# Two biases of a deformable-convolution block: three-row products on TensorE, or an add on VectorE as the products are copied to SBUF

## The chip, the cores and the metric

The kernel runs on one core of one Trainium2 chip. The metric is the time of one execution on the device in microseconds. Before the change it was 2654.45 us, the median of three runs (2650.62 to 2654.76).

## The reference

One layer with a deformable convolution, an attention layer and an expert layer, over x of 8 x 56 x 56 x 128 in fp32. The change touches the end of the first:

```python
y = dcn_core(xp, offset, mask) @ w_out + b_out
x = x + gamma1 * layer_norm(y, ln1_g, ln1_b)
m = gelu(x @ w_fc1 + b_fc1) @ w_fc2 + b_fc2
x = x + gamma2 * layer_norm(m, ln2_g, ln2_b)
```

Then causal self-attention over the 3136 tokens of an image (128 wide) is added to x, and then a layer of 64 experts, each of which takes the 8 tokens of an image with the largest gate values.

## The kernel before

**Work and order.** Each image's tokens are cut into four groups of 896 or 448 tokens, 7 or 4 tiles of 128 (the last of a 448 group half full); there are 32 groups. A group passes through some twenty *lines* of steps, written as generators: `prepare` (transposes, the input product), `conv` (depthwise taps on VectorE, L576), `plan` and `weigh` (tap weights; their product with the sampled rows on VectorE, L715), `sums` (folds of these products on GpSimd, L732), `project`, `norm`, `scores`, `maxes` (score evictions on VectorE, L1092), `exps`, `turn`, `pour`, `attend`, `mix` and `after`. All lines of all groups are interleaved by one long string, `ORDER`: each letter advances one line by one step, and the steps' instructions are put on the engines' queues in that order. Each engine works its queue in order. The string came out of a search by a planner, which works with the costs in `need(engine, us, ...)`; `lock=True` marks VectorE steps that it takes to exclude GpSimd. On the chip these costs do nothing. After the last `project` the experts' tiles take the place of the first stage's; the experts' products and the scatters to the output close the program.

**`project`.** A group's tiles are taken in banks of three or four (one PSUM bank of 512 columns). For each bank:

1. `py` = bias + yT x `w_out`, in the PSUM tile `held` (L841: the bias; L843: one product for each tile, which runs as two instructions).
2. `add_normed`, through `deviations`: ScalarE squares each tile of `py` with a sum over the columns (L784), GpSimd makes of the sums the reciprocal standard deviations (L786 and `power`, L775), ScalarE scales the tiles into `u` (L796), TensorE transposes them (L801), VectorE scales and adds them to `xT` (L803).
3. The two layers of 512: products with `fc1` (L856) and GELU (L863); then `pm` = bias + products with `fc2`, again in `held` (L875: the bias; L877).
4. `deviations` of `pm`; for each tile VectorE multiplies it with its deviation and with `grow`, the row of gains, into `u` (L897); VectorE adds `u` to the transposed `xT` and stores it in `t` (L907).

The means need no step: `settle` takes the mean over the columns off `w_out`, `fc2` and both biases beforehand (`centered`). It also splits each bias into three bf16 rows whose sum is the fp32 value (L442, L443, L446); the bias comes into PSUM as a product of these three rows with three rows of ones:

```python
nc.tensor.matmul(py[:, : m * C], three, b_out[:, : m * C], start=True, stop=False)
```

There are 7 banks to an image, 56 in all, of which 24 hold three tiles and 32 four; and 200 tiles. Other lines that will be named: L543, where VectorE adds the bias of the input product as it copies that product from PSUM to SBUF; L1240, which adds the attention's result to `t`; L1387 and L1477, which add gathered rows up in SBUF, weighted; L1406, L1378, L621, L645 and L648, small VectorE steps on tiles in SBUF; L1140, the exponential of the scores in SBUF; L1998, the load of a bias row to many partitions near the end.

## Time and profile before

| | |
|---|---|
| runs | 2654.76, 2654.45, 2650.62 us |
| profiled execution | 2649.75 us, span 2647.7 us |
| mean granted TensorE clock | 0.979 |
| DMA | 442.63 MB, mean 167 GB/s |
| tap products (L715) | 200 x 3.48 us on VectorE |
| folds (L732) | 1075 on GpSimd, 1419.7 us |
| products of the attention (L1203) | 5200 instructions, 681.4 us on TensorE |

The profile shows one execution of the program. The span runs from its first instruction to its last; the execution's time is 2.05 us longer. Busy times are of the engine's own instructions; a wait for a semaphore ahead of an instruction is not part of them, but what an instruction waits for after it has begun is. In a line of a group stand: line, engine, operation, out<-in by the program's names, out<-in sizes, how many; then busy us, mean ns of one; then how long the engine stood idle just before them, and what ended most of that. In a line of the waits stand: who waited, for whom, us in total, times, longest us. A line of the program in order of time begins with its start and its length in us.

### The profile page before, as it was taken

How to read it: one execution, taken by the hardware profiler on the slowest of the kernel's cores; microseconds unless marked ns; L12 is line 12 of the kernel's file. 1: busy time of each engine (PE TensorE's matmuls, PEld its weight loads, DVE VectorE, ACT ScalarE, POOL GpSimd, SP SyncE). 2: the span in 40 equal slices, each digit the busy share in tenths (PEclk: the TensorE clock that was granted, in tenths of full speed). 3: DMA queues.
4: the chain of work that ended last, by engine and by line, in shares of the span. 5: the costliest groups of instructions: out<-in, count | busy, mean ns of one | idle time of the engine just before them, and what ended most of it. 6: DMA issues, size and time to landing. Idle time of an engine off the chain costs nothing. (4 is left out here: it accounts for less than half of the span.)

```text
span 2647.7 us, 47634 instructions
## 1 busy us (share of the span) xinstructions
PE 2467.3 (93%) x16297; PEld 1883.2 (71%) x16297; DVE 2166.3 (82%) x4661; ACT 1943.2 (73%) x4524; POOL 2179.0 (82%) x2315
## 2 busy tenths in 40 slices
PE   4789999999999999999999899999999999999975
PEld 3677777777776778777776667766777777777744
DVE  6988877899898987888889897888889988765553
ACT  2356787888787887888778577977888887876630
POOL 3686889889998899989899899987998899882245
PEclk9799999999999999999999999999999999999987
DMA  5665544544553454444454354544465445335083
GB/s 163 204 226 203 203 169 159 193 129 164 188 187 124 161 193 176 173 150 167 169 182 153 123 199 170 181 149 151 160 202 172 146 167 191 132 94 197 23 280 117
DMA packets 274296, 442.63 MB, mean 167 GB/s; under 512 B 14332, under 2 KB 127356, under 8 KB 274044
## 3 DMA queue, kind: packets, MB, share of 16 engines
q1 hardware_dynamic: 184220, 382.09, 41.2%
q10 hardware_dynamic: 86464, 50.94, 6.3%
q0 software_dynamic: 3360, 6.45, 0.8%
q8 instruction: 132, 2.16, 0.3%
q14 instruction: 120, 0.98, 0.1%
HBM read 386.04 MB, written 53.48 MB: 166 GB/s over the span
## 5 line engine op out<-in xcount | busy, mean ns | idle before, releaser
L732 POOL TENSOR_TENSOR g<-g 128x128 f32<-128x128 f32 (+6 forms) x1075 | 1419.7, 1329 | 104.0 <-DVE g L715 25.4
L715 DVE TENSOR_TENSOR g<-g,tp 128x3200 f32<-128x3200 f32 (+1 forms) x200 | 695.2, 3478 | 17.7 <-ACT tp L706 10.8
L1203 PEld LDWEIGHTS av<-v,pe 128*128 128x128 f32 (+2 forms) x5200 | 626.4, 188 | 97.3 <-issue 60.1
L1203 PE MATMUL av<-v,pe 128*128 128x129 f32 (+2 forms) x5200 | 681.4, 277 | 2.8 <-ACT pe L1173 1.5
L1066 PE MATMUL sc<-zT,qT 128*128 128x384 f32 (+8 forms) x1622 | 657.7, 516 | 16.9 <-DVE S L1092 8.2
L1092 DVE TENSOR_SCALAR_CACHE_REDUCE S<-sc 128x512 f32<-128x512 f32 (+5 forms) x783 | 443.4, 576 | 209.5 <-PE sc L1066 121.8
L1140 ACT ACTIVATE S<-S,low 128x512 f32<-128x512 f32 (+5 forms) x783 | 478.7, 638 | 42.9 <-DVE low L1108 31.1
L1173 ACT COPY pe<-tr 128x512 f32<-128x512 f32 (+3 forms) x775 | 379.8, 500 | 143.9 <-PE tr L1158 111.1
L1158 PE MATMUL tr<-ident,S 128*128 128x128 f32 x2516 | 392.5, 276 | 12.6 <-DVE S L1092 9.5
L1158 PEld LDWEIGHTS tr<-ident,S 128*128 128x128 f32 x2516 | 297.4, 142 | 130.3 <-issue 68.5
L1066 PEld LDWEIGHTS sc<-zT,qT 128*128 128x128 f32 (+1 forms) x1622 | 247.0, 187 | 113.2 <-issue 43.4
L576 DVE SCALAR_TENSOR_TENSOR pv<-xg,dw,pv 128x448 f32<-128x448 f32 x448 | 305.8, 683 | 14.0 <-ACT pv L573 8.3
L877 PEld LDWEIGHTS pm<-fc,hid 128*128 128x128 f32 x1600 | 200.3, 193 | 37.7 <-issue 22.6
L877 PE MATMUL pm<-fc,hid 128*128 128x128 f32 x1600 | 222.4, 282 | 1.5 <-POOL hid L862 1.0
L856 PE MATMUL ph<-xT,fc 128*128 128x512 f32 (+2 forms) x448 | 207.4, 551 | 6.0 <-DVE xT L803 4.0
L863 ACT ACTIVATE hid<-ph,b_fc 128x512 f32<-128x512 f32 (+2 forms) x224 | 140.7, 633 | 97.0 <-PE ph L856 93.9
L667 POOL TENSOR_TENSOR taps<-taps,a 128x252 f32<-128x252 f32 (+1 forms) x288 | 191.3, 664 | 8.8
L657 POOL TENSOR_TENSOR a<-w 128x756 f32<-128x756 f32 (+1 forms) x96 | 136.4, 1420 | 20.9 <-DVE w L648 18.4
L1140 ACT ACT_TABLE_LOAD x87 | 111.6, 1283 | 6.0 <-DVE pv L576 3.7
L760 ACT COPY ys<-ptg 128x128 f32<-128x128 f32 (+1 forms) x200 | 52.4, 262 | 84.9 <-PE ptg L749 43.0
L749 PE MATMUL ptg<-ident,g 128*128 128x128 f32 (+1 forms) x650 | 85.0, 292 | 25.1 <-POOL g L732 25.0
L749 PEld LDWEIGHTS ptg<-ident,g 128*128 128x128 f32 (+1 forms) x650 | 81.8, 207 | 29.2 <-POOL g L732 27.6
(328 smaller groups left out, 3716.0 us busy)
## 6 DMA issues: line engine op xcount, KB each, us to landing
g<-img SPq DMA_DIRECT2D x192, 1600.0 KB
w1t<-in_L_ffn_weight_dram SPq DMA_DIRECT2D x32, 512.0 KB
w2t<-in_L_ffn_weight_dram SPq DMA_DIRECT2D x32, 512.0 KB
xin<-in_x_dram SPq DMA_DIRECT2D x56, 224.0 KB
xTd<-xc ACTq DMA_DIRECT2D x56, 224.0 KB
img<-st ACTq DMA_DIRECT2D x112, 112.0 KB
out_dram<-t ACTq DMA_DIRECT2D x24, 448.0 KB
g<-img SPq DMA_DIRECT2D x8, 800.0 KB
```

Source lines behind the costliest of these rows:

```text
L576: nc.vector.scalar_tensor_tensor(p3, src, dw[:, k : k + 1], p3, op0=ALU.mult, op1=ALU.add)
L667: nc.gpsimd.tensor_add(dst, dst, a5[:, :nt, kx])
L715: nc.vector.tensor_mul(g3, g3, tp[:n, lt % 4].unsqueeze(2).to_broadcast([n, NTAP * NG, 32]))
L732: nc.gpsimd.tensor_add(g[:n, o * C : (o + w) * C], g[:n, o * C : (o + w) * C], g[:n, i * C : (i + w) * C])
L856: nc.tensor.matmul(ph[:, :n], fc1[:, f * P : (f + 1) * P], xT[:, :n], start=True, stop=True)
L877: nc.tensor.matmul(four(pm, m)[:, i, :], h[:, i * P : (i + 1) * P], fc2[:, f, :], start=False, stop=i == m - 1 and f == 3,)
L1066: nc.tensor.matmul(pp[h * HALF : h * HALF + qw, c0 : c0 + m], qT[:, q0 : q0 + qw], zTs[b, g][:, k0 : k0 + m], start=True, stop=not seg.las ...
L1092: nc.vector.tensor_scalar(S[p0:p1, c0:c1], pp[p0:p1, c0:c1], -SCALE, None, ALU.mult, ALU.min, accum_out=(mn[p0:p1, i, j + k : j + k + 1] i ...
L1140: nc.scalar.activation(S[p0:p1, c0:c1], S[p0:p1, c0:c1], AF.Exp, bias=low[p0:p1, i : i + 1], scale=-1.0)
L1158: nc.tensor.transpose(pt[:m, k + p0 : k + w], S[p0:w, k : k + m], ident[p0:w, p0:w])
L1173: nc.scalar.copy(pe[:, : full * P], pt[:, : full * P])
L1203: nc.tensor.matmul(p3[h * HALF : h * HALF + qw, i % 3, :], pe[:kw, k + h * HALF : k + h * HALF + qw], vs[b, g][:kw, (k0 + k - c0) // P, :] ...
```

## The change

`raw_b` holds both biases in fp32 on all 128 partitions. The three-row products, and what prepares them, are gone. After `py` is done, and again after `pm`, a new step `biased` adds the bias on VectorE and writes `y` in SBUF; Square and the scaling on ScalarE, and the multiply by `grow` on VectorE, read `y` where they read PSUM. `u` is now `y` itself, in place; the squares go to a tile of their own. `ORDER` is another string throughout.

```diff
 ORDER = (
-    "ppppbpppppppwbpwwpppwvvfvvvvvvvvbppwcpccccckpwcccpccpccpbpppwfccwvccvccvccvvvccvwwcccvfvcgvg"
...
+    "ppppbppppppwpwpppwpvvvvvvbvvbvvpwcppwcbcccccfppcwwcccpppcpcpvwcvvwcccvvwvcccwvcvcvfvvcvwfvvb"
...
-    raw_b = wk.tile([3, 2, C], F32, tag="oT", name="raw_b")
+    raw_b = sp.tile([P, 2, C], F32, tag="b3", name="raw_b")
     for k, n in enumerate(("L0_conv_b_out", "L0_conv_b_fc2")):
-        nc.sync.dma_start(raw_b[:, k], a[n].partition_broadcast(3))
+        nc.sync.dma_start(raw_b[:, k], a[n].partition_broadcast(P))
...
-    three = cst.tile([3, P], BF16, tag="three", name="three")
-    nc.gpsimd.memset(three, 1.0)
-    less = cst.tile([3, 2], F32, tag="less", name="less")
-    nc.gpsimd.memset(less, -1.0)
-    nc.gpsimd.memset(less[:1, 0:1], 0.0)
-    nc.gpsimd.memset(less[:2, 1:2], 0.0)
-    b3 = sp.tile([3, 2, 4 * C], BF16, tag="b3", name="b3")
-    b_out, b_fc2 = b3[:, 0], b3[:, 1]
...
         for k in range(2):
             yield need(DVE, 1.4)
-            v = raw_b[:, k]
-            centered(v, 3, 5 + k)
...
+            centered(raw_b[:, k], P, 5 + k)
...
     def deviations(pb, name):
...
-        u = sp.tile([P, 4, C], F32, tag="u", name="u" + name)
         for i in range(m):
-            nc.scalar.activation(u[:, i], pb[:, i, :], AF.Square, accum_out=ss[:, i : i + 1])
+            square = sp.tile([P, C], F32, tag="square", name=f"square{name}_{i}")
+            nc.scalar.activation(square, pb[:, i, :], AF.Square, accum_out=ss[:, i : i + 1])
...
-        return ss, u
+        return ss
...
     def add_normed(xT, pb, name):
...
-        ss, u = yield from deviations(pb, name)
+        ss, u = (yield from deviations(pb, name)), pb
...
+    def biased(pb, k, m, name):
+
+        yield need(DVE, 0.15 + 0.135 * m)
+        y = sp.tile([P, 4, C], F32, tag="y", name="y" + name)
+        nc.vector.tensor_add(y[:, :m], four(pb, m), raw_b[:, k].unsqueeze(1).to_broadcast([P, m, C]))
+        return y[:, :m]
...
-            yield need(PE, 0.22 + 0.224 * m, since=[there, None])
+            yield need(PE, 0.115 * m, since=[there, None])
             py = ps.tile([P, 512], F32, tag="held", name=f"py{nm}_{i0}")
-            nc.tensor.matmul(py[:, : m * C], three, b_out[:, : m * C], start=True, stop=False)
             for i in range(m):
                 nc.tensor.matmul(
                     four(py, m)[:, i, :],
                     yT[:, (i0 + i) * P : (i0 + i + 1) * P],
                     w_out,
-                    start=False,
-                    stop=i == m - 1,
-                )
-            yield from add_normed(xT[:, :n], four(py, m), f"a{nm}_{i0}")
+                    start=True,
+                    stop=True,
+                )
+            y = yield from biased(py, 0, m, f"a{nm}_{i0}")
+            yield from add_normed(xT[:, :n], y, f"a{nm}_{i0}")
...
-                turned[f] = yield need(PE, 0.224 * m + 0.22 * (f == 0), since=at)
+                turned[f] = yield need(PE, 0.224 * m, since=at)
...
-                    nc.tensor.matmul(pm[:, : m * C], three, b_fc2[:, : m * C], start=True, stop=False)
...
-                        start=False,
+                        start=f == 0 and i == 0,
...
-            ss, u = yield from deviations(four(pm, m), f"b{nm}_{i0}")
+            y = yield from biased(pm, 1, m, f"b{nm}_{i0}")
+            ss, u = (yield from deviations(y, f"b{nm}_{i0}")), y
             for i in range(m):
                 yield need(DVE, 0.345)
                 nc.vector.scalar_tensor_tensor(
                     u[:, i, :],
-                    four(pm, m)[:, i, :],
+                    y[:, i, :],
                     ss[:, i : i + 1],
                     grow,
```

## The prediction

> **What bounds the kernel now.** I read the busy shares first, then the table by stage, then the groups of the operations that the change touches, then single instructions in order of time. The shares over the whole span:

> ```profile
> PE 2467.3 (93%) x16297; PEld 1883.2 (71%) x16297; DVE 2166.3 (82%) x4661; ACT 1943.2 (73%) x4524; POOL 2179.0 (82%) x2315
> ```

> The first bias product starts at 97 us and the last at 2394 us, so the stretch that counts is 100 to 2400 us. The table by stage gives, after the stretch's limits and length, the busy time of TensorE, its weight loads, VectorE, ScalarE and GpSimd, then the granted clock. The second and third lines are the two 100 us stages in which VectorE was busiest.

> ```profile
> 100.00:2400.00 2300.00, 2224.00 (x14373) 1697.85 (x14373) 1963.57 (x4113) 1808.38 (x4240) 2038.26 (x2107) 0.99 0.49 168
> 100.00:200.00 100.00, 87.41 (x599) 72.93 (x598) 92.29 (x116) 49.82 (x136) 78.28 (x70) 0.94 0.63 224
> 2000.00:2100.00 100.00, 96.27 (x639) 72.43 (x638) 92.11 (x229) 80.58 (x197) 88.22 (x99) 1.00 0.42 138
> ```

> TensorE is busy for 2224/2300 = 96.7% of it: it is the bound, at a granted clock of 0.99. VectorE stands at 85.4% and GpSimd at 88.6%, not far behind, and no 100 us stage shows VectorE above 92.3%. The chain that ended last shows only the final scatters and says nothing of this stretch.

> **The change, part by part.** There are 7 banks to an image, 56 in all; 24 hold three tiles and 32 hold four, 200 tiles together. Each bank passes both layer norms.

> *Products taken off TensorE.* 112 three-row products go. Their groups (busy us, mean ns of one, idle before them):

> ```profile
> L875 PE MATMUL pm<-b,three 3*128 3x512 bf16 x32 | 12.5, 391 | 0.0
> L841 PE MATMUL py<-b,three 3*128 3x512 bf16 x32 | 12.5, 391 | 0.6 <-DVE ub L897 0.6
> ...
> L875 PE MATMUL pm<-b,three 3*128 3x384 bf16 x24 | 7.9, 331 | 0.0
> L841 PE MATMUL py<-b,three 3*128 3x384 bf16 x24 | 7.9, 331 | 0.7 <-DVE ub L897 0.7
> ```

> That is 2 x (12.5 + 7.9) = 40.8 us of TensorE, all on the bounding engine, so 41 us is the most that the change can win. The bank `held` comes free sooner; TensorE waited 0.6 + 0.7 us for that, which I cost at nothing.

> *Adds put on VectorE.* Each reads a product from PSUM and a bias row from SBUF and writes SBUF. That is the form of L543, and nearly that of L907, so the second and the fourth of these lines price it. The other two price a thing that the diff does in passing: the multiply by `grow` (L897) reads `y` in SBUF where it read `pm` in PSUM, so that both its tensors now lie in SBUF. L1387 is the same operation at the same size with both in SBUF.

> ```profile
> L897 DVE SCALAR_TENSOR_TENSOR ub<-pm,ssb,grow 128x128 f32<-128x128 f32 x200 | 59.4, 342 | 28.8 <-POOL ssb L775 28.8
> ...
> L543 DVE TENSOR_TENSOR st<-pq,b_in 114x512 f32<-114x512 f32 x56 | 38.3, 684 | 25.7 <-PE pq L538 25.5
> ...
> L1387 DVE SCALAR_TENSOR_TENSOR po<-gx,chances,po 128x128 f32<-128x128 f32 x21 | 21.0, 999 | 0.0
> ...
> L907 DVE TENSOR_TENSOR t<-ub,pt 128x384 f32<-128x384 f32 x32 | 17.6, 549 | 0.5
> ```

> The adds: 2 x (32 x 0.684 + 24 x 0.549) = 70.1 us.

> *The multiply.* L897 takes 342 ns and L1387 takes 999. In order of time the reason stands side by side (start us, us):

> ```profile
> 862.06 1.12 DVE L897 SCALAR_TENSOR_TENSOR ub<-pm,ssb,grow 128x128 f32<-128x128 f32 x4
> 863.09 2.84 DVE L1387 SCALAR_TENSOR_TENSOR po<-gx,chances,po 128x128 f32<-128x128 f32 x1
> ```

> ```profile
> 862.35 3.44 POOL L732 TENSOR_TENSOR g<-g 128x1536 f32<-128x1536 f32 x1
> ```

> Four multiplies with a PSUM operand run through a GpSimd fold undisturbed. The one with two SBUF operands ends at 865.93, with the fold (865.79). Its shortest is 337 ns, its median 529, its longest 3341: the work is no longer, it waits for GpSimd's instruction in flight. GpSimd is busy for 88.6% of the stretch, and right ahead of these multiplies, since they follow its `pow`. Price: 200 x (0.999 - 0.342) = 131.4 us of VectorE. Bounds: at the end, where GpSimd has little to do, the same form (L1477) takes 411 ns on average, which makes 200 x 0.069 = 14 us; if each waits for a mean GpSimd instruction (2179.0/2315 = 0.94 us), 188 us. I take 131, the row with the same form, engine and stage. GpSimd in turn: a 128x128 fold right behind such a multiply (855.42 us) took 507 ns against a mean of 460, so 200 x 0.05 = 10 us; if each multiply held it for its whole length, 68 us.

> [...]

> *ScalarE.* Square and the scaling read SBUF, not PSUM. A 512-wide activation takes 725 ns from SBUF (L1140) and 686 from PSUM (L863): 600 x 39 ns = 23 us, on an engine with 78.6% of the stretch. I cost it at nothing; uncovered it is 23 us.

> [...]

> *The wait that is added.* Square waited for TensorE and now waits for the add, which stands in VectorE's queue among score evictions (L1092), convolution taps (L576) and tap products (L715); behind Square wait the two small GpSimd steps. GpSimd already stands idle for it:

> ```profile
> POOL ssb L786 <- ACT ub L784: 61.3, 29, 9.8
> ```

> The other lines' work hides one more step of 0.6 us in each of 112 norms as long as VectorE is on time. I cost it at nothing; without cover it is 112 x 0.63 = 70 us.

> *The start.* `raw_b` comes in over 128 partitions instead of 3, on SP's queue in its old place; a like broadcast load near the end took SP 1.9 to 3.2 us to issue (L1998), so at most 5 us later for what stands behind it. Five GpSimd memsets and 4.8 us of VectorE's splitting (1.4 + 2.3 + 1.1) go. TensorE is busy for 45 of the first 100 us and waits for other things: nothing either way.

> *The order.* All engines' queues get another order. Nothing in the trace prices that. It can win at most TensorE's idle time of the stretch, 76 us, and I bound a loss by the same; I take zero and keep some 40 us on each side for the range. What speaks for the losing side: the planned costs of the new code give the multiply 0.345 us with no lock, and the `py` product 0.115 us a tile where L843 was busy for 60.5 us over 200 tiles, 0.30 each.

> **The sum.** VectorE in the stretch: 1963.6 + 70.1 + 131.4 = 2165 us, 94.1% of 2300. Two ways on from there.

> By capacity: the busiest stages show 92%. At 92% throughout, 2165 us need 2353 us, +53; at 90%, 2406, +106.

> By what reaches TensorE: 1460 to 1490 us is a place with many such waits.

> ```profile
> 1460.00:1490.00 30.00, 23.08 (x131) 15.80 (x129) 27.52 (x48) 18.37 (x46) 28.39 (x29) 1.00 0.43 136
> ```

> ```profile
> L1406 DVE TENSOR_SCALAR slot_f<-at_f 32x8 f32<-32x8 f32 x4 | 4.1, 1021 | 0.1
> ...
> L645 DVE TENSOR_TENSOR om<-om,red 128x252 f32<-128x252 f32 x1 | 3.5, 3458 | 0.0
> ```

> Besides these five, L621 took 2.55 us and L1378 2.28. Undisturbed they take 0.16 us (the shortest L1406, taken for L1378 too) and 0.42 (the median L645, taken for L621 too), so the seven lost 3.4 + 3.0 + 2.1 + 2.1 = 10.6 us. TensorE was busy for 23.1 us where its mean share gives 29.0: 5.9 lost, 0.56 of the wait. So 0.56 x 131.4 = +74. The adds are no waits and alone would bring VectorE to 88.4%: nothing. Of the 41 us saved I count half, because TensorE now waits for VectorE more often: -20. Sum +54.

> The two ways give +53 to +106. I take +60: the profiled execution (2649.75 us, span 2647.7) becomes 2709.8, and as it lies 4.7 us below the median of the runs, the median becomes 2714.

> **The rivals.**
> *VectorE becomes the bound outright* (10%): each multiply waits for a whole GpSimd instruction (+188) and the queue reaches only 90%: (1963.6 + 70 + 188)/0.9 = 2469, +169, some 2820. For it: four multiplies run in a row, and the next fold can get in between them. Against: L1387 runs between other work too and shows a median of 529.

> *Faster* (16%): the multiplies meet GpSimd in its pauses, or between short steps, as L1477 does with 411 ns. VectorE then carries 70 + 14 us more, 88.9%, TensorE stays the bound and gives back 40.8 x 0.967 = 39 us: 2615. It decides for this side where the mean of the 200 multiplies stays below about 0.45 us. Against it: GpSimd has 11% of the stretch free, and the multiply follows GpSimd's own step.

> *Gain and loss cancel* (4%): about half the price of the waits, within 0.2% of before, which is about what a measurement of this kernel can tell from no change. That the products stay is excluded: the diff deletes them.

> **How the numbers follow.** Slower as forecast 70%, VectorE as the bound 10%: slower 0.80; same 0.04; faster 0.16. The main case by itself reaches from 2660 (a good order) to 2775 (+106 and some of the order). From 2625 to 2810 the range leaves out most of the fastest rival and the upper half of the slowest, under 2 in 10.

> **What would show it.** The multiply's group: about 1.0 us on average with a shortest of 0.34, many ending with a GpSimd fold; the adds at 0.68 and 0.55 without spread; VectorE near 2365 us in all and above 92% in many stages; TensorE 41 us less busy, but more of its idle time ended by VectorE. Wrong if the multiply's mean is below 0.45 us, or if VectorE holds 94% and TensorE does not slow.

## The result, and the profile after

The changed kernel takes 2785.4 us (median of four runs, 2784.15 to 2786.36) against 2652.8 us before: 132.6 us more, a ratio of 1.0509 with an interval of 1.0496 to 1.0521. The forecast was +60. The direction and the mechanism that it named are there; the size is more than twice what it gave. The profiled execution took 2785.58 us (span 2783.7), at a mean granted clock of 0.962 where it was 0.979.

The busy shares of the changed kernel:

```profile
PE 2479.5 (89%) x16185; PEld 1904.4 (68%) x16185; DVE 2363.3 (85%) x4763; ACT 1993.8 (72%) x4524; POOL 2190.0 (79%) x2311
```

VectorE did 197 us more, within 2 us of the 2365 us that the prediction worked out. TensorE has the 112 products fewer (x16185 for x16297), but instead of 41 us less it was busy for 12 us *more*. That is the line to be puzzled by: fewer instructions, more time. Its idle time grew from 180.4 us (2647.7 - 2467.3) to 304.2.

The table by stage of the changed kernel, same columns as before; the second and third line are the two 100 us stages with the busiest VectorE:

```profile
100.00:2550.00 2450.00, 2249.46 (x14318) 1727.20 (x14319) 2168.82 (x4247) 1869.13 (x4263) 2050.88 (x2110) 0.97 0.46 158
200.00:300.00 100.00, 91.23 (x620) 75.12 (x619) 92.79 (x137) 58.40 (x142) 65.44 (x52) 0.97 0.53 189
700.00:800.00 100.00, 94.08 (x615) 73.40 (x615) 93.22 (x172) 78.75 (x180) 91.73 (x89) 1.00 0.50 175
```

VectorE carries 2168.82 us of its stretch, but the stretch has grown with it: 88.5% of 2450, not the 94.1% of the old length. Four of the 24 stages from 100 to 2500 us lie above 92% (before: two), where the prediction looked for many. No engine is full; the kernel is slower although every engine but VectorE has more room than before.

The groups of the multiply and of the four-tile adds after the first product (busy us, mean ns of one, idle before them):

```profile
L886 DVE SCALAR_TENSOR_TENSOR yb<-yb,ssb,grow 128x128 f32<-128x128 f32 x200 | 222.9, 1157 | 18.7 <-POOL ssb L757 17.5 <-ACT pe L1162 1.2
...
L801 DVE TENSOR_TENSOR ya<-py,raw_b 128x512 f32<-128x512 f32 x32 | 21.9, 686 | 17.2 <-PE py L831 17.0
```

The adds are as priced: 0.69 us here and 0.55 for three tiles, all between 0.54 and 0.70. With the pair after `pm` they take 70.3 us. The multiply is not: 1157 ns on average where 342 stood, with a shortest of 311, a median of 754 and a longest of 3593. Of the 200, 150 took over 450 ns, and each of those ended within 0.16 us behind the end of a GpSimd instruction (median 0.15).

The longest waits show who is late now:

```profile
POOL ssa L768 <- ACT squarea L766: 117.3, 40, 8.6
...
POOL ssb L768 <- ACT squareb L766: 65.0, 38, 7.3
```

Before, the second stood at 61.3 us and the first here:

```profile
POOL ssa L786 <- ACT ua L784: 41.3, 23, 7.3
```

TensorE's own waits rose from 152.7 to 275.2 us; those ended by VectorE from 54 to 127.5.

**One such wait from start to end.** VectorE, the changed kernel, in order of time (start us, us):

```profile
905.84 1.37 DVE L886 SCALAR_TENSOR_TENSOR yb<-yb,ssb,grow 128x128 f32<-128x128 f32 x1
...
907.20 6.42 DVE L886 SCALAR_TENSOR_TENSOR yb<-yb,ssb,grow 128x128 f32<-128x128 f32 x3
913.54 0.68 DVE L1081 TENSOR_SCALAR_CACHE_REDUCE S<-sc 128x512 f32<-128x512 f32 x1
```

GpSimd in the same microseconds:

```profile
905.51 1.55 POOL L639 TENSOR_TENSOR a<-w 128x756 f32<-128x756 f32 x1
907.03 7.39 POOL L714 TENSOR_TENSOR g<-g 128x1536 f32<-128x1536 f32 x5
```

TensorE behind them:

```profile
908.61 0.81 PE L1055 MATMUL sc<-zT,qT 128*128 128x384 f32 x2
...
909.92 0.49 PE L1147 MATMUL tr<-ident,S 128*128 128x128 f32 x3
914.28 1.65 PE L1055 MATMUL sc<-zT,qT 128*128 128x384 f32 x2 [3.87 <-DVE S L1081]
```

The first multiply ends just behind GpSimd's `a` product, and the next three wait among its five folds: 7.8 us for what takes 1.4 undisturbed. The score eviction (L1081) queued behind them comes late, and TensorE, which waits for it, stands for 3.87 us. Then comes the part that the prediction did not see: the same two score products that took 0.81 us take 1.65. The table by stage of the same place says why (the granted clock is the sixth figure behind the stage's length, those in brackets not counted):

```profile
910.00:914.20 4.20, 0.41 (x4) 0.17 (x2) 4.20 (x6) 1.02 (x2) 3.96 (x5) 0.86 0.41 159
914.20:921.00 6.80, 6.72 (x22) 4.04 (x23) 6.12 (x22) 4.13 (x14) 3.15 (x7) 0.59 0.00 0
921.00:926.00 5.00, 5.00 (x28) 3.27 (x28) 3.78 (x12) 2.77 (x5) 4.92 (x3) 1.00 0.61 225
```

Behind the pause TensorE is "busy" for 6.72 of 6.80 us at a clock of 0.59, with 22 instructions where the 5 us after it hold 28. The pause is paid twice: once as idle time, and once as a stretch at half speed (a granted clock of 0.50 until 919.83 us) that counts as busy.

### The profile page after: what moved, and what is told of

It is laid out like the page before. It is cut to its first block, busy times and chain, and to the rows that moved or that the text cites. A ratio compares the mean times of both kernels' runs of the same rounds, so it can differ in the third digit from the quotient of the medians.

```text
span 2783.7 us, 47363 instructions
## 1 busy us (share of the span) xinstructions
PE 2479.5 (89%) x16185; PEld 1904.4 (68%) x16185; DVE 2363.3 (85%) x4763; ACT 1993.8 (72%) x4524; POOL 2190.0 (79%) x2311
## 5 line engine op out<-in xcount | busy, mean ns | idle before, releaser
L1055 PE MATMUL sc<-zT,qT 128*128 128x384 f32 (+8 forms) x1622 | 675.3, 526 | 64.2 <-DVE S L1081 32.4
L1192 PEld LDWEIGHTS av<-v,pe 128*128 128x128 f32 (+2 forms) x5200 | 637.9, 191 | 109.3 <-issue 57.7
L1192 PE MATMUL av<-v,pe 128*128 128x129 f32 (+2 forms) x5200 | 694.2, 280 | 8.7 <-ACT pe L1162 7.8
L1081 DVE TENSOR_SCALAR_CACHE_REDUCE S<-sc 128x512 f32<-128x512 f32 (+5 forms) x783 | 442.7, 576 | 146.8 <-PE sc L1055 97.6
L1147 PE MATMUL tr<-ident,S 128*128 128x128 f32 x2516 | 402.2, 279 | 45.3 <-DVE S L1081 13.1
L886 DVE SCALAR_TENSOR_TENSOR yb<-yb,ssb,grow 128x128 f32<-128x128 f32 x200 | 222.9, 1157 | 18.7 <-POOL ssb L757 17.5
L865 PE MATMUL pm<-fc,hid 128*128 128x128 f32 x1600 | 215.5, 278 | 3.2 <-ACT hid L852 2.8
L852 ACT ACTIVATE hid<-ph,b_fc 128x512 f32<-128x512 f32 (+2 forms) x224 | 141.2, 634 | 67.9 <-PE ph L845 64.5
L731 PE MATMUL ptg<-ident,g 128*128 128x128 f32 (+1 forms) x650 | 91.3, 306 | 27.2 <-POOL g L714 26.0
```

What stands on the lines that cost most here:

```text
L865: nc.tensor.matmul(four(pm, m)[:, i, :], h[:, i * P : (i + 1) * P], fc2[:, f, :], start=f == 0 and i == 0, stop=i == m - 1 and f == 3,)
L886: nc.vector.scalar_tensor_tensor(u[:, i, :], y[:, i, :], ss[:, i : i + 1], grow, op0=ALU.mult, op1=ALU.mult,)
L1055: nc.tensor.matmul(pp[h * HALF : h * HALF + qw, c0 : c0 + m], qT[:, q0 : q0 + qw], zTs[b, g][:, k0 : k0 + m], start=True, stop=not seg.las ...
L1081: nc.vector.tensor_scalar(S[p0:p1, c0:c1], pp[p0:p1, c0:c1], -SCALE, None, ALU.mult, ALU.min, accum_out=(mn[p0:p1, i, j + k : j + k + 1] i ...
L1147: nc.tensor.transpose(pt[:m, k + p0 : k + w], S[p0:w, k : k + m], ident[p0:w, p0:w])
L1192: nc.tensor.matmul(p3[h * HALF : h * HALF + qw, i % 3, :], pe[:kw, k + h * HALF : k + h * HALF + qw], vs[b, g][:kw, (k0 + k - c0) // P, :] ...
```

## The experiments

The theory: the multiply's second SBUF operand makes it wait for GpSimd, and that alone costs most of the time. The rivals: the new order is worse whatever it orders (prediction: zero, within 40 us); the adds load VectorE until it is the bound.

**e1: the change without the lock.** The changed kernel in its own order; the sum after `pm` goes back into PSUM, and the multiply reads it there.

```diff
+        kept = four(pb, m) if k else y[:, :m]
-        nc.vector.tensor_add(y[:, :m], four(pb, m), ...)
-        return y[:, :m]
+        nc.vector.tensor_add(kept, four(pb, m), ...)
+        return kept, y[:, :m]
...
-            y = yield from biased(pm, 1, m, f"b{nm}_{i0}")
-            ss, u = (yield from deviations(y, f"b{nm}_{i0}")), y
+            y, u = yield from biased(pm, 1, m, f"b{nm}_{i0}")
+            ss = yield from deviations(y, f"b{nm}_{i0}")
```

> The changed kernel in its own order; the second add writes its sum back into the PSUM bank it read, so that Square and the multiply by grow read PSUM and the multiply has one SBUF operand. The adds, the missing products and the order stay. Theory of the lock: the multiplies fall from 1157 to about 342 ns, VectorE to about 2200 us busy, and most of the 131 us lost comes back: 2640 to 2680 us. Theory of the order (another string, planned with too small costs): the multiplies get shorter too, but the time stays above 2740 us. Theory of the load (VectorE has 70 us of adds more): above 2720 us.

Measured: 2661.8 us against 2649.8 before, a ratio of 1.0042 (1.0028 to 1.0057). The page's shares and the multiply's group of this kernel:

```profile
PE 2440.9 (92%) x16185; PEld 1880.2 (71%) x16185; DVE 2206.2 (83%) x4763; ACT 1984.4 (75%) x4524; POOL 2184.7 (82%) x2311
```

```profile
L887 DVE SCALAR_TENSOR_TENSOR yb<-pm,ssb,grow 128x128 f32<-128x128 f32 x200 | 59.5, 342 | 16.3 <-POOL ssb L757 14.8 <-ACT S L1130 1.3
```

Same order, same adds; the one difference is which memory holds the second sum, which Square and the multiply read. The multiply is back at 342 ns, and 123.6 us are gone. (Before itself took 2649.8 us beside this run and 2652.8 beside the changed kernel. Each against its own, the loss falls from 132.6 to 12.0 us, by 120.6.) What the change does on purpose, in the order made for it, costs 12 us; what it does in passing costs ten times that.

**e2: the lock without the change.** Before's code and order; only the multiply's first operand moves to SBUF. It reads the squares that lie there, so the values of the second norm are others; the same holds for e6 and e7.

```diff
                 nc.vector.scalar_tensor_tensor(
                     u[:, i, :],
-                    four(pm, m)[:, i, :],
+                    u[:, i, :],
```

> The kernel before, order and three-row products included; only the multiply by grow reads the squares, which lie in SBUF, in place of the product in PSUM (the values of the second norm are thereby others). Theory of the lock: multiplies of 1.0 to 1.2 us, VectorE about 2310 us busy, time 2730 us by the 0.56 of the prediction, 2760 us or more if the stalls also bring TensorE's clock down. Theories of the order and of the load: no more than 2680 us.

Measured: 2789.1 us, 1.0525 (1.0507 to 1.0542). The page's shares and the group:

```profile
PE 2512.5 (90%) x16297; PEld 1913.2 (69%) x16297; DVE 2315.8 (83%) x4661; ACT 1943.7 (70%) x4524; POOL 2183.4 (78%) x2315
```

```profile
L897 DVE SCALAR_TENSOR_TENSOR ub<-ub,ssb,grow 128x128 f32<-128x128 f32 x200 | 216.7, 1126 | 20.1 <-POOL ssb L775 20.1
```

One word of the program, and the whole loss is there: +139 us, for 200 x (1.126 - 0.342) = 157 us of waits. In the profiled executions the span grew by 134 us (2647.7 to 2781.9). That splits into 89 us more of TensorE idle (180.4 to 269.4) and 45 us more of TensorE busy, with the same 16297 instructions. So 89/157 = 0.57 of the waits reached TensorE as idle time, next to the 0.56 of the prediction, and the 45 us come on top. VectorE stands at 83% of the span: it is not the bound.

**e3: the order alone.** Before's code, three-row products and all, in the new `ORDER`, with an empty step where the adds have theirs:

```diff
-ORDER = ( ...before... )
+ORDER = ( ...after... )
...
+            yield need(DVE, 0.0)
```

> The code of before, three-row products included, in the order of after; the steps of the adds are empty. Theory of the order: 2730 us or more. Theories of the lock and of the load: 2640 to 2670 us. Multiplies at 342 ns, TensorE's own work as before, so what is longer comes from the order alone.

Measured: 2684.7 us, 1.0122 (1.0105 to 1.0139): +34.8 us. The page's shares:

```profile
PE 2480.8 (92%) x16297; PEld 1892.2 (70%) x16297; DVE 2168.3 (81%) x4661; ACT 1945.4 (72%) x4524; POOL 2186.2 (81%) x2315
```

TensorE was busy for 13.5 us more than before; the rest is its idle time. With e1 the swap of products for adds in the new order is 2661.81 - 2684.65 = -22.8 us; TensorE's busy time falls from 2480.8 to 2440.9, by 39.9. That is close to the prediction's 40.8 and to the half of it, -20, that it let reach the end.

**e4 and e5: the adds in the old order.** The change with before's string; the add stands in `deviations`, right ahead of the squares, since the old string has no letter for it. In e5 the sum after `pm` is kept in PSUM as in e1.

```diff
-    def deviations(pb, name):
+    def deviations(pb, k, name):
...
+        y = sp.tile([P, 4, C], F32, tag="y", name="y" + name)[:, :m]
+        nc.vector.tensor_add(y, pb, raw_b[:, k]...)      # e4
+        kept = pb if k else y                             # e5
+        nc.vector.tensor_add(kept, pb, raw_b[:, k]...)    # e5
```

> All of the changed code, adds and SBUF operands, in the order of before; each add is queued on VectorE where the squares of its bank were queued on ScalarE. Theory of the lock: 2770 us or more, since the old order knows no more of the waits than the new one does. Theory of the order: 2700 us or less.

> The order of before; adds in place of the three-row products, each queued on VectorE where its bank's squares are queued on ScalarE; the second sum goes back to PSUM, so that the multiply stays at 342 ns. Against e4 this takes away the lock alone. Theory of the lock, with nothing else at work: 2630 to 2680 us (41 us of TensorE won, 70 us of VectorE's idle time used). Theory that an add which the order has no place for stalls VectorE's queue: 2720 us or more, and then the lock's price in e4 (2957 us) is some 140 to 240 us on top.

Measured: e4 2956.8 us, 1.1154 (1.1135 to 1.1172); e5 2788.9 us, 1.0528 (1.051 to 1.0546). So the adds without the lock, which with the new order cost 12 us (e1), cost 138 us where the string does not provide for them. (One place for them in the old order was tried; another may cost less.) How late Square comes shows the difference. Worked out from the traces, from the end of a bank's product to the start of its first Square, as a mean over the 112 norms: in the old order 0.77 us before and 2.09 in e5; in the new order 1.88 in e3 and 2.26 in e1. In the new order Square stands later anyway, and the add pushes it back by 0.4 us; in the old one it pushes it back by 1.3 us, twice the 0.63 that an add takes. The waits of e5:

```profile
POOL ssb L771 <- ACT squareb L769: 130.3, 47, 11.8
POOL ssa L771 <- ACT squarea L769: 85.6, 41, 7.9
```

Together 216 us, against 103 before and 112 in e1. (They are not a measure of the adds alone: in e2, without an add, they are 173 us.) This is the wait that the prediction cost at nothing "as long as VectorE is on time" and at 70 us uncovered; in e5 the loss is twice that. VectorE has 80% of the span in e5, so this too is a matter of waiting and not of capacity.

**e6: the lock in the new order.** e3 with the edit of e2.

```diff
-                    four(pm, m)[:, i, :],
+                    u[:, i, :],
```

> e3 (the code of before in the order of after, three-row products and no adds) with the multiply reading the squares in SBUF (the values of the second norm are thereby others). If the lock costs the same whatever surrounds it, 2685 + 120 to 140 = 2805 to 2825 us. If the new order had room for it, below 2760 us.

Measured: 2788.4 us, 1.0511 (1.0492 to 1.0531). A miss: the lock costs 104 us here, not the 120 to 140 expected, for 165 us of waits:

```profile
L900 DVE SCALAR_TENSOR_TENSOR ub<-ub,ssb,grow 128x128 f32<-128x128 f32 x200 | 224.7, 1166 | 15.1 <-POOL ssb L776 13.5 <-ACT pe L1176 1.3
```

The price of a wait depends on the order and the work around it. The four pairs that differ in the lock alone:

| | without the lock | with it | difference |
|---|---|---|---|
| old order, products | 2650 (before) | 2789 (e2) | +139 |
| new order, products | 2685 (e3) | 2788 (e6) | +104 |
| new order, adds | 2662 (e1) | 2785 (after) | +124 |
| old order, adds | 2789 (e5) | 2957 (e4) | +168 |

**e7: a quarter of the lock.** Before, with only the first multiply of each bank reading SBUF; it tells whether four in a row do the harm, or each wait for itself.

```diff
-                    four(pm, m)[:, i, :],
+                    four(pm, m)[:, i, :] if i else u[:, i, :],
```

> The kernel before; only the first multiply of each bank reads the squares in SBUF (the values of those tiles in the second norm are thereby others), 56 of 200. If each wait counts by itself, a little over a quarter of e2's 139 us: 2685 to 2695 us. If the first multiply of a run waits and the others follow it without a wait, most of the loss: above 2740 us. If waits cost only when they pile up, 2650 to 2665 us.

Measured: 2685.7 us, 1.0137 (1.012 to 1.0154). Both forms of the multiply in one kernel:

```profile
L897 DVE SCALAR_TENSOR_TENSOR ub<-ub,ssb,grow 128x128 f32<-128x128 f32 x56 | 65.9, 1176 | 27.2 <-POOL ssb L775 27.0
...
L897 DVE SCALAR_TENSOR_TENSOR ub<-pm,ssb,grow 128x128 f32<-128x128 f32 x144 | 43.2, 339 | 0.0
```

56 of 200 is 28%, and the loss is 35.2 us, 25% of e2's 139. So each wait counts roughly by itself: 0.83 us of waiting, 0.63 us of the kernel's time.

**e8 and e9: other locked steps taken away from before.** If waits for GpSimd cost 0.6 to 0.9 of their length, taking away those that before already has should win. e8 moves two small offsets (L1317 and L1406) to ScalarE; e9 in addition puts the maximum of the masks (L619) into free columns of a PSUM tile, so that L621 has one SBUF operand.

```diff
-        nc.vector.tensor_scalar_add(ci[:, k8], cu[half_], float(...))
+        nc.scalar.activation(ci[:, k8], cu[half_], AF.Copy, bias=float(...))
...
-        nc.vector.tensor_reduce(red, mk...)
+        top = po[:, 512 - GT * NG :]...                   # e9
+        nc.vector.tensor_reduce(top, mk...)               # e9
```

> The kernel before, less two of the waits that it already has: the offset added to the indices (L1317, 31 steps of 809 ns on average with a shortest of 163) and the slots (L1406, 16 of 529 with a shortest of 152) move from VectorE to ScalarE, each to the start of the ScalarE step that follows it anyway. VectorE loses some 33 us, of which 26 us were waits for GpSimd; ScalarE gets about 10 us. Theory of the lock, at 0.66 to 0.89 of a wait: 17 to 23 us faster than before, 2627 to 2635 us. If waits of an order that was searched with them are already covered: 2645 to 2655 us. If ScalarE's queue stalls on the indices: slower than before.

> e8, and the largest mask value of each group of taps (L619) is written to unused columns of the PSUM bank that the offsets came in, so that the subtraction (L621, 32 steps, about 20 us of waits) has one operand in SBUF; the bank comes free two VectorE steps later. Theory of the lock: L621 falls to about 0.4 us, and the time by another 13 to 18 us. If the bank is missed: slower than e8.

Measured, on a chip where before took 2692.5 us, so that only the differences count: e8 2686.1 us, 0.9978 (0.9969 to 0.9987), -6.4; e9 2683.2 us, 0.9963 (0.9949 to 0.9977), -9.2. In e9 the step that took 1148 ns:

```profile
L622 DVE TENSOR_TENSOR om<-om,po 128x252 f32<-128x252 f32 x24 | 9.8, 410 | 0.3
```

The steps that were aimed at lost what was planned: e8 took 33.6 us of them off VectorE, e9 another 20.7. In e8 other steps of VectorE took longer, so that its busy time fell by 22.5 us only; in e9 it fell to 2117.8 us, 48 less than in the trace of before (which is from another chip). The time followed only by a fifth: e8 missed its 17 to 23 us, e9 won 3 us more, not 13 to 18. So the price of a wait that was put in is not what one gets back for a wait taken out. e9 beats before by 0.4% all the same. That the order was searched with these waits in place, so that what follows them is not ready any sooner, is a likely reason, but no run here shows it.

## Why the prediction was right or wrong

By its own steps:

- *Adds, +70.1 us of VectorE:* 70.3. Right, from the row of the same form. That they alone reach nothing holds in the new order only (e1); in the old one they cost 138 us (e5).
- *Multiply, +131.4 us:* 163.5 (222.9 - 59.4), 0.82 us a wait instead of 0.66. Mis-sized, inside its bounds of 14 and 188. The row taken (L1387, 999 ns) was of the right form. A likely reason, which no run isolates, is that the multiply stands right behind GpSimd's own step and comes in runs of three or four, so that it meets GpSimd more often. That VectorE's sum came out at 2363 all the same is luck: adds and multiply together brought 233.8 us, but its busy time rose by 197.0, since other steps took less, among them L1387 (21.0 to 15.5 us), L1406 (8.5 to 3.5) and the large forms of L621, L645 and L648 (98.5 to 73.8), whose small forms took more (22.4 to 37.7).
- *What reaches TensorE, 0.56:* this is the step that failed. As a share of idle time it was in the middle of what the four pairs show: 0.57 in e2, (304.2 - 220.2)/163.4 = 0.51 from e1 to after, 0.36 from e3 to e6, 0.68 from e5 to e4. But the sum took idle time for the whole price and left the granted clock out. From e1 to after TensorE's busy time grows by 38.6 us with the same 16185 instructions; in e2 by 45.2. By the medians the lock costs 0.76 of its waits in after, 0.89 in e2, 0.63 in e6 and 0.98 in e4. So 0.56 x 131.4 = 74 us stood where 124 were measured, some 84 of them idle time and 39 the slower clock.
- *By capacity, +53 to +106:* the second way, which the prediction let stand beside the first, took VectorE as the limit at 90 to 92%. It stood at 88.5%, and the time went into waits.
- *The order, zero:* +34.8 with the old code (e3), near the end of the 40 us kept for it, and with the swap's -22.8 it leaves +12 for everything but the lock, where the prediction had -20.
- *GpSimd +10 us:* +4.4 by the lock alone (e2). After has +11.0, of which 7.2 come with the order (e3).
- *ScalarE +23 us, hidden:* +50.6. Square with the reads of its sums went from 115.4 to 160.7 us, the scaling from 57.8 to 64.5. A Square took 309 ns for 277 and a scaling 393 for 373, about as priced. The rest is that the Squares of a bank follow one another more slowly: one began 0.25 us after the one ahead of it in the kernel before, 0.43 us in after, and 0.40 in e1 for `pm`, where Square reads PSUM as it did. So most of it does not come from the memory that Square reads. The change also has all Squares write to one small buffer, `square`, in turn; whether that is the cause, no run tests. Hidden as said: e1 has 1984.4 us of it and only 12 us more time.
- *TensorE 41 us less busy:* seen only from e3 to e1 (39.9). In after the clock took it back.

The sum in measured differences: order +34.8, swap -22.8, waits +123.6, together +135.6. It divides the loss and is no check of it, since its steps lead from before by e3 and e1 to after. The 3 us to the +132.6 of the result are the difference between the two times of before.

The warning stood in the trace of before, in the ten microseconds behind the sample from which the 0.56 came. Table by stage of the kernel before:

```profile
1490.00:1500.00 10.00, 8.03 (x37) 6.78 (x38) 4.40 (x15) 3.96 (x7) 1.29 (x1) 0.66 0.09 26
```

TensorE's pause began in the sample, at 1487.31 us, and ended behind it, at 1491.97, and then the clock was down: the sample was cut in the middle of the bill. The clock of 0.66 is worth 0.34 x 10 = 3.4 us more, and TensorE was busy for 8.0 us where its mean share gives 9.7. With the 5.9 us of the sample that is 10.9 us for the 10.6 us of waits, instead of 0.56 of them. (The list of seven waits also leaves out L1375, which took 0.90 us there and 0.15 elsewhere.) One place is a rough sample, but the clock was there to be read.

Whether the clock explains all of TensorE's extra busy time can be checked in every kernel. Worked out from the granted clock of the traces, over the stretches at half clock that begin between 100 us and 250 us before the end: the time at half clock (0.50 in the records), half of its excess over before's 27 us, and beside it TensorE's busy time over before's (over before's less 40.8 where the products are gone):

| | half clock, us | half of the excess | TensorE's extra busy time |
|---|---|---|---|
| e1 | 55 | 14 | 14.4 |
| e3 | 55 | 14 | 13.5 |
| e7 | 58 | 15 | 12.0 |
| e5 | 99 | 36 | 49.1 |
| e2 | 126 | 50 | 45.2 |
| after | 140 | 56 | 53.0 |
| e6 | 150 | 61 | 57.2 |
| e4 | 249 | 111 | 107.5 |

Eight kernels from 12 to 108 us, seven within 5 us of the estimate and e5 13 us above it, which stays open. That the waits bring the clock down is shown by e2, which adds nothing else. That a given drop comes from the pause just ahead of it is read from the traces; the last section has the counts.

The rivals. "VectorE becomes the bound outright" gave some 2820 us, and the time lies between it and the main case, but the mechanism is not that one: 83% of the span in e2 and 80% in e5, with the same time at both. "Faster" had as its point of decision a mean below 0.45 us for the multiply. e1, at 342 ns, shows that even there the change in this order, but for where the second sum lies, does not win: 1.0042, not the forecast 2615. The order costs 35 us by itself and takes up more than the swap wins.

## What to carry to other kernels

Before an operand is moved from PSUM to SBUF in a VectorE step with another SBUF operand, ask what GpSimd does at that moment: here the same multiply took 342 ns from PSUM and 1157 from SBUF, and keeping the sum in PSUM saved some 120 us with the rest of the change in place. A stall of TensorE is priced over its idle time and the ten microseconds behind it, with the granted clock read there: where it fell here, it stood at 0.50 for 3.4 or 6.8 us. And a static order is part of the code: the same 70 us of adds cost 12 us with the other edits in an order made for them, and 138 in one that was not.

## What was not expected of the hardware

**Half clock behind short pauses.** The changed kernel, table by stage, a pause of 2 us:

```profile
1914.50:1916.50 2.00, 0.01 (x1) 0.00 (x0) 2.00 (x4) 1.92 (x4) 1.84 (x4) 1.00 1.02 393
1916.50:1920.00 3.50, 3.46 (x12) 2.66 (x13) 2.95 (x9) 1.21 (x2) 0.34 (x1) 0.51 0.53 207
```

**GpSimd hardly pays.** In e2 a multiply that takes 0.34 us in before lasts up to 3.7 us, and the 200 of them waited 157 us in all. GpSimd, for which the prediction's upper bound was 68 us, lost 4.4 there: the waiting was nearly all on one side. One reason, which no run isolates, may be that a multiply that had waited ended only 0.15 us behind GpSimd's instruction (the median in after), so that little of its 0.34 us was left to hold up the next.
